# Selective scans: B written to DRAM with zeros between its values and read back as diagonal matrices for three of eight token tiles, the other five scaled on ScalarE

## The chip, the core and the metric

The program runs on one core of one Trainium2 chip. That core has TensorE (PE, with its weight loads shown as PEld), VectorE (DVE), ScalarE (ACT), GpSimd (POOL) and SyncE (SP). SP computes nothing here; it issues the DMAs of the scans, one after the other. The metric is the device time of one execution in microseconds (us), the median of several runs. Profiles are of one execution each.

## What is computed

The input is an image of 256 x 256 tokens with 128 channels. A triangle attention layer comes first, then a layer with a selective scan. Only the scans are touched here:

```python
def step(h, inp):
    d_t, x_t, B_t, C_t = inp
    dA = jnp.exp(d_t[..., None] * As)
    h = dA * h + (d_t * x_t)[..., None] * B_t[:, :, None, :]
    y = jnp.einsum('bkdn,bkn->bkd', h, C_t)
    return (h, y)
```

There are K = 4 scans over L = 65,536 tokens (along the rows and along the columns, each forwards and backwards). Every scan has D_INNER = 256 channels and D_STATE = 16 states, so for each state n the kernel needs, per channel and token, the decay `dA`, the input `d*x*B[n]`, the recurrence, and the product with `C[n]`.

## The kernel before

The function `scans` cuts each scan into 64 blocks of TB = 1024 tokens, so there are 256 blocks. A block has NJ = 8 token tiles of P = 128 tokens. The 256 channels are two halves (h = 0, 1). A block is worked off in 32 steps: s = 2m + h, with m the state. In each step

- `recur` (L853) runs one recurrence over 128 channels x 1024 tokens on DVE (L858). At h = 1 it also takes the last state (L863, DVE) and multiplies both halves by C on POOL (L865, two instructions), for which `cc`, one row of C spread over 128 partitions, has come by DMA.
- `turn` (L841) makes the input of the next step on PE. The product `d*x` is at hand as `dxt`, with tokens on partitions. The scan wants channels on partitions and the product with B[n], which is one number per token. So for tiles 0 to 3 PE multiplies `dxt` with a 128 x 128 matrix `dg` that has B on its diagonal (L846; an f32 product is two passes, so eight matmul records), and for tiles 4 to 7 it transposes `but`, which is `dxt` already multiplied by B (L848; four records). The result lies in one of two PSUM buffers `mm`, which alternate. A buffer is free when the DVE instruction that reads it has ended.
- `scale` (L830) makes what `turn` will need six steps later, on ACT: two `dg` (identity times B, L833) and two `but` (L835) per step. Both have rings of four, one buffer for each m modulo 4.
- `decay` (L837) makes exp(delta * A) on ACT for four steps later (L839), in a ring of six.
- `collect_some` (L882) turns the products with C back with PE transposes that accumulate in PSUM (the helper in L617), three states behind; `evict` (L893) adds them to y on DVE in steps 6 and 8 of the next block (L898).
- `fetch` (L825), at h = 1, has SP issue the DMA of the `cc` of state m + 4. It waits until POOL has done state m, which read the buffer before.

Beside its own steps a block prepares the next one: `begin` (L737) returns a list of pieces, each with a step and a mark for before or after that step's own work, and `advance` issues them. Steps 6, 8, 18 and 20 have `rate` (PE, L750, with a wait for a `mm` buffer); steps 6 to 12 have six wide activations on ACT (L759 to L774), steps 11 to 14 four instructions on POOL (`log1p` L780, `less` L777), steps 18 and 20 `softplus` on DVE (L783), steps 22 and 24 `turn_rate` (PE, L790) with `times_x` (DVE, L794). At the start of a block SP issues the next block's `bt` (B, 64 KB) and `xk` (1 MB); in step 8 it stores y (L902, 1 MB), in step 16 it loads the next y (L948, 1 MB), in step 21 it loads `dt` (32 KB).

The scans stand under `tc.manual_schedule()`, so every engine works off its instructions in the order in which the Python code issues them. The DMAs of the scans are all on SP's one queue: SP waits for whatever a DMA needs before it issues it, and what stands behind it on SP waits too. Eighteen blocks form the body of a hardware loop, which is run three times for each scan; the other ten blocks of a scan are written out.

Of the kernel before, what the change touches and what calls it, by code (L numbers as in the profile page):

```python
# [29 lines left out]
AF = mybir.ActivationFunctionType  # L30
# [5 lines left out]
P = 128  # L36
# [4 lines left out]
DI = 256  # L41
NH = DI // P
DS = 16
# [576 lines left out]
def scans(tc, io, c):  # L620
# [11 lines left out]
    nc = tc.nc  # L632
    TB = 1024
    NJ = TB // P
# [5 lines left out]
    with tc.tile_pool(name="e_w", bufs=1) as wp, tc.tile_pool(name="e_1", bufs=1) as sb1, tc.tile_pool(  # L640
# [11 lines left out]
        def ring(name, n, shape, pool=wp):  # L652
            return [pool.tile(shape, F32, name=f"{name}{i}") for i in range(n)]

        DJ = NJ // 2
        xks = ring("xk", 1, [P, NJ, DI])

        dts = ring("dt", 1, [P, TB])
# [4 lines left out]
        ybs = ring("yb", 1, [P, NJ, DI])  # L663
        ccs = ring("cc", 4, [P, TB])
        dgs = ring("dg", 4, [P, DJ, P])
        bus = ring("but", 4, [P, NJ - DJ, DI])
        das = ring("da", DA, [P, TB])
        hss = ring("hs", HS, [P, NH, TB])
        mms = ring("mm", 2, [P, TB], psum)
# [3 lines left out]
        def mm():  # L673
            count[0] += 1
            return mms[count[0] % 2]
# [9 lines left out]
        class Block:  # L685
# [40 lines left out]
            def load_tokens(self):  # L726
                nc.sync.dma_start(out=self.as_rows(self.bt), in_=self.rows(io["bk"][self.S.k]))
                nc.sync.dma_start(out=self.as_rows(self.xk), in_=self.rows(io["xk"]))

            def advance(self, now, after):  # L730
                if self.pieces is None:
# [5 lines left out]
        def begin(B):  # L737


            k = B.S.k  # L740
            B.pu, B.e = {}, None

            def rate(h):
                if B.e is None:
                    B.e = sb1.tile([P, NH, TB], F32, name="e")
                pu = B.pu[h] = mm()
                for q in range(0, TB, T):
                    nc.tensor.matmul(  # L750
                        pu[:, q : q + T],
                        dtw[0 : DR + 1, k, h * P : (h + 1) * P],
                        B.dt[0 : DR + 1, q : q + T],
                        start=True,
                        stop=True,
                    )

            def size(h):
                nc.scalar.activation(B.e[:, h, :], B.pu[h], AF.Abs)  # L759

            def exp():
                nc.scalar.activation(B.e, B.e, AF.Exp, scale=-1.0)

            def log():
                B.lw = sb1.tile([P, NH, TB], F32, name="lw")
                nc.scalar.activation(B.lw, B.e, AF.Ln, bias=1.0)  # L766

            def one_plus():
                B.w = sb1.tile([P, NH, TB], F32, name="w")
                nc.scalar.activation(B.w, B.e, AF.Identity, bias=1.0)  # L770

            def rest():

                nc.scalar.activation(B.w, B.w, AF.Identity, scale=-1.0, bias=1.0)  # L774

            def less(h):
                nc.gpsimd.tensor_tensor(B.lw[:, h, :], B.lw[:, h, :], B.w[:, h, :], ALU.add)  # L777

            def log1p(h):
                nc.gpsimd.tensor_tensor(B.lw[:, h, :], B.lw[:, h, :], B.e[:, h, :], ALU.add)  # L780

            def softplus(h):
                nc.vector.scalar_tensor_tensor(B.delta[:, h, :], B.pu[h], 0.0, B.lw[:, h, :], ALU.max, ALU.add)  # L783

            def turn_rate(i):
                B.pt = mm().rearrange("p (j d) -> p j d", d=DI)
                for j in range(NJ // 2):
                    for h in range(NH):
                        at = (i * NJ // 2 + j) * P
                        nc.tensor.transpose(B.pt[:, j, h * P : (h + 1) * P], B.delta[:, h, at : at + P], c.ident)  # L790

            def times_x(i):
                G = N // P
                nc.vector.tensor_tensor(  # L794
                    B.dxt[:, i * NJ // 2 : (i + 1) * NJ // 2, :].rearrange("p (w g) c -> p w g c", g=G),
                    B.pt.rearrange("p (w g) c -> p w g c", g=G),
                    B.in_order(B.xk, i, 2),
                    ALU.mult,
                )

            return [
                (6, False, rate, 0),
                (6, True, size, 0),
                (8, False, rate, 1),
                (8, True, size, 1),
                (9, True, exp),
                (10, True, log),
                (11, True, log1p, 0),
                (11, True, one_plus),
                (12, True, log1p, 1),  # L810
                (12, True, rest),
                (13, True, less, 0),
                (14, True, less, 1),

                (18, False, rate, 0),
                (18, True, softplus, 0),
                (20, False, rate, 1),
                (20, True, softplus, 1),
                (22, False, turn_rate, 0),
                (22, True, times_x, 0),  # L820
                (24, False, turn_rate, 1),
                (24, True, times_x, 1),
            ]

        def fetch(B, m):  # L825
            nc.sync.dma_start(out=ccs[m % 4], in_=B.S.C[m : m + 1, B.where()].partition_broadcast(P))

        def scale(B, m, h):  # L830
            dg, bu = dgs[m % 4], bus[m % 4]
            for j in range(h * DJ // 2, (h + 1) * DJ // 2):
                nc.scalar.activation(dg[:, j, :], c.ident, AF.Copy, scale=B.bt[:, B.slot(j), m : m + 1])  # L833
                at = B.slot(DJ + j)
                nc.scalar.activation(bu[:, j, :], B.dxt[:, DJ + j, :], AF.Copy, scale=B.bt[:, at, m : m + 1])  # L835

        def decay(B, m, h):  # L837
            da = das[((B.n * DS + m) * NH + h) % DA]
# [2 lines left out]
        def turn(B, m, h):  # L841
            d1 = B.d1 = mm()
            dg, bu = dgs[m % 4], bus[m % 4]
            hc = slice(h * P, (h + 1) * P)
            for j in range(DJ):
                nc.tensor.matmul(d1[:, j * P : (j + 1) * P], B.dxt[:, j, hc], dg[:, j, :], start=True, stop=True)  # L846
            for j in range(DJ, NJ):
                nc.tensor.transpose(d1[:, j * P : (j + 1) * P], bu[:, j - DJ, hc], c.ident)  # L848
            d1s.append(d1)

        d1s = []
# [56 lines left out]
        def body(blocks, before, after):  # L908
# [8 lines left out]
            def at(u):  # L917
                x, s = divmod(u, U)
                return (at_hand[x], *divmod(s, NH)) if x in at_hand else None

            def do(f, u):
                if at(u):
                    f(*at(u))

            if before is None:
                blocks[0].load()
                blocks[0].load_tokens()
                blocks[0].advance(U, True)
                blocks[0].free = set(range(NJ // PB))
                blocks[1].load()  # L930
                for m in range(4):
                    fetch(blocks[0], m)
                for u in range(3 * NH):
                    do(scale, u)
                for u in range(4):
                    do(decay, u)
                do(turn, 0)
            for x, B in enumerate(blocks):
                nxt = at_hand.get(x + 1)
                for s in range(U):  # L940
                    u = x * U + s
                    m, h = divmod(s, NH)
                    if s == 0 and nxt:
                        nxt.load_tokens()
                    if s == 21 and x + 2 in at_hand:
                        at_hand[x + 2].load()
                    if s == 16:
                        nc.sync.dma_start(out=B.as_rows(B.y), in_=B.rows(io["y"]))  # L948
                    if nxt:
                        nxt.advance(s, False)  # L950
                    recur(B, m, h)
                    do(turn, u + 1)
                    if at(u - LAG * NH):
                        waiting.extend((*at(u - LAG * NH), j) for j in range(NJ))
                    collect_some(len(waiting) if s == LAG * NH - 1 else share.get(s, 10))
                    if x - 1 in at_hand and s in (6, 8):
                        evict(at_hand[x - 1], B, (s - 6) // 2)
                    if nxt:
                        nxt.advance(s, True)
                    do(decay, u + 4)  # L960
                    if u == 0:
                        nc.scalar.preload_act_table_set("natural_log_exp_and_others")
                    do(scale, u + 3 * NH)
                    if h == NH - 1 and at(u + 1 + 3 * NH):
                        fetch(*at(u + 1 + 3 * NH)[:2])
            if not after:
# [9 lines left out]
        first = (n - passes * LOOP) // 4 * 2  # L976
# [21 lines left out]
def output(tc, io, c):  # L998
# [73 lines left out]
    "dc1": (KD // 2 * RC, NT),  # L1072
    "dcT": (KD // 2 * RC, NT),
    "y": (NT, DI),
}


# [56 lines left out]
```

## Time and profile before

| | |
|---|---|
| time, median of 3 runs | 28445.06 us (28438.65 to 28445.41) |
| the profiled execution, span | 28447.5 us |
| TensorE clock granted, mean | 0.965 |
| scans: L846 first at 4,768 us, last L858 at 27,653 us | some 22,890 us for 256 blocks, 89.4 each |
| busy share PE / DVE / ACT / POOL, whole span | 94% / 88% / 89% / 81% |
| DMA queue of the scans (q1) | 3339.77 MB, 34.6% of 16 engines |

The shares are means over the whole program: attention, convolution and output stand in them too. A share near the top says that an engine is rarely idle, and not that it sets the pace: an engine that waits a little at each step and one that is waited for look much alike there. What sets the pace is read from which engine has no gap in a stretch, and from what ends the gaps of the others. DMA rows give what moved and for how long; a row of the timeline gives start, length, engine, line and the instruction, with the idle time before it and what ended that in brackets.

### The profile page before, as it was taken

The numbers are of one execution on the slowest core, as the hardware profiler recorded it, in microseconds if no ns is written. First come the engines' busy times: TensorE is split into PE (matmuls) and PEld (weight loads), VectorE is DVE, ScalarE is ACT, GpSimd is POOL, SyncE is SP. The second block draws the span as 40 slices with busy tenths as digits, with TensorE's granted clock in tenths as the row PEclk, the third lists the DMA queues.
The fourth block names the chain that finished last, engine by engine and source line by source line (L and its number), as shares of the span: only waits on it lengthen the run. The fifth ranks groups of instructions, "written<-read, shape, count | busy, mean of one in ns | idle before, by whom it ended". The sixth has DMA issues, their size and how long they took to land. (4 is left out here: it accounts for less than half of the span.)

```text
span 28447.5 us, 528099 instructions
## 1 busy us (share of the span) xinstructions
PE 26610.1 (94%) x196490; PEld 22529.2 (79%) x196490; DVE 24922.2 (88%) x24253; ACT 25332.4 (89%) x49673; POOL 22944.4 (81%) x10118
## 2 busy tenths in 40 slices
PE   8999996999999999999999999999999999999998
PEld 3555444888888888888888888888888888888884
DVE  4777665999999999999999999999999999999987
ACT  6875224999999999999999999999999999999987
POOL 2443002999999999999999999999999999999983
PEclk9999998999999999999999999999999999999999
DMA  5112345433433333333334333333333333333335
GB/s 206 55 50 71 111 116 115 132 132 129 133 130 133 132 131 132 132 131 132 128 132 133 131 133 132 131 132 129 132 132 130 133 132 129 132 130 132 133 132 172
DMA packets 1923996, 3630.07 MB, mean 128 GB/s; under 512 B 532297, under 2 KB 1240009, under 8 KB 1889490
## 3 DMA queue, kind: packets, MB, share of 16 engines
q1 hardware_dynamic: 1424722, 3339.77, 34.6%
q10 hardware_dynamic: 496640, 255.88, 3.2%
q8 instruction: 1568, 25.69, 0.4%
q14 instruction: 1066, 8.73, 0.1%
HBM read 3002.42 MB, written 592.84 MB: 126 GB/s over the span
## 5 line engine op out<-in xcount | busy, mean ns | idle before, releaser
L865 POOL TENSOR_TENSOR hs<-hs,cc 128x1024 f32<-128x1024 f32 x8192 | 19202.5, 2380 | 1346.1 <-DVE state L863 679.9
L858 DVE TENSOR_TENSOR_SCAN hs<-da,state,mm 128x1024 f32<-128x1024 f32 x8192 | 18976.6, 2340 | 1465.4 <-PE mm L848 1074.7
L846 PE MATMUL mm<-dg,dxt 128*128 128x128 f32 x65536 | 9305.0, 287 | 1065.1 <-DVE hs L858 886.1
L846 PEld LDWEIGHTS mm<-dg,dxt 128*128 128x128 f32 x65536 | 8328.4, 199 | 2257.9 <-DVE hs L858 1897.8
L839 ACT ACTIVATE da<-delta,A 128x1024 f32<-128x1024 f32 x8192 | 9328.4, 1139 | 112.2 <-PEq L984 76.0
L617 PE MATMUL y<-ident,hs 128*128 128x128 f32 x65536 | 8511.4, 275 | 1.4 <-POOL hs L865 1.4
L835 ACT ACTIVATE but<-dxt,bt 128x256 f32<-128x256 f32 x16384 | 8150.2, 497 | 11.4 <-DVE dxt L794 11.4
L617 PEld LDWEIGHTS y<-ident,hs 128*128 128x128 f32 x65536 | 7494.1, 143 | 1.9 <-POOL hs L865 1.9
L833 ACT ACTIVATE dg<-ident,bt 128x128 f32<-128x128 f32 x16384 | 6393.1, 390 | 0.2
L848 PE MATMUL mm<-ident,but 128*128 128x128 f32 x32768 | 5092.5, 280 | 0.0
L848 PEld LDWEIGHTS mm<-ident,but 128*128 128x128 f32 x32768 | 4011.4, 146 | 0.0
L750 PE MATMUL mm<-dt,dtw 9*128 9x512 f32 x4096 | 2033.0, 615 | 265.9 <-DMA bt<-mid_bk 184.5
L385 POOL TENSOR_TENSOR an<-ex,rs 128x1024 f32<-128x1024 f32 x512 | 970.2, 1895 | 1024.5 <-PE tp L394 566.3
L780 POOL TENSOR_TENSOR lw<-lw,e 128x1024 f32<-128x1024 f32 x512 | 1207.7, 2384 | 336.3 <-ACT lw L766 336.3
L750 PEld LDWEIGHTS mm<-dt,dtw 9*128 9x128 f32 x4096 | 680.7, 184 | 959.5 <-issue 733.3
L500 POOL MEMSET pad<- 128x10 f32 x32 | 3.7, 117 | 1650.0 <-PE ps L537 1639.9
L777 POOL TENSOR_TENSOR lw<-lw,w 128x1024 f32<-128x1024 f32 x512 | 1202.9, 2375 | 0.0
L537 PE MATMUL ps<-pad,w 128*128 128x512 f32 x2048 | 954.8, 610 | 161.0 <-ACT xi L525 161.0
L372 ACT ACTIVATE ex<-sc,nm 128x256 f32<-128x256 f32 x2048 | 1013.7, 499 | 0.4
L759 ACT ACTIVATE e<-mm 128x1024 f32<-128x1024 f32 x512 | 524.7, 1025 | 522.1 <-PE mm L750 521.9
L355 DVE CUSTOM_DVE_ANT_0 sc<-ps,bias 128x256 f32<-128x256 f32 x2048 | 746.2, 421 | 117.3 <-PE ps L340 117.3
L394 PEld LDWEIGHTS tp<-ident,an 128*128 128x128 f32 x4096 | 467.5, 141 | 470.7 <-POOL an L385 235.1
(137 smaller groups left out, 18522.4 us busy)
## 6 DMA issues: line engine op xcount, KB each, us to landing
cc<-mid_dc SPq DMA_DIRECT2D x2048, 512.0 KB
cc<-mid_dcT SPq DMA_DIRECT2D x2048, 512.0 KB
xk<-mid_xk SPq DMA_DIRECT2D x256, 1024.0 KB
yb<-mid_y SPq DMA_DIRECT2D x256, 1024.0 KB
mid_y<-yb SPq DMA_DIRECT2D x256, 1024.0 KB
xt<-mid_xT SPq DMA_DIRECT2D x64, 1024.0 KB
mid_xk<-xk ACTq DMA_DIRECT2D x32, 2048.0 KB
mid_y<-y ACTq DMA_DIRECT2D x32, 2048.0 KB
```

Of the source, the lines that this page charges most:

```text
L372: nc.scalar.activation(exs[u][:, x, :], scs[u][:, e, jt, :], AF.Exp, scale=-1.0, bias=nms[u][:, e, jt : jt + 1], accum_out=sms[u][:, x : x ...
L617: nc.tensor.matmul(out, in_, c.ident, is_transpose=True, start=start, stop=stop, skip_group_check=True)
L750: nc.tensor.matmul(pu[:, q : q + T], dtw[0 : DR + 1, k, h * P : (h + 1) * P], B.dt[0 : DR + 1, q : q + T], start=True, stop=True,)
L777: nc.gpsimd.tensor_tensor(B.lw[:, h, :], B.lw[:, h, :], B.w[:, h, :], ALU.add)
L780: nc.gpsimd.tensor_tensor(B.lw[:, h, :], B.lw[:, h, :], B.e[:, h, :], ALU.add)
L833: nc.scalar.activation(dg[:, j, :], c.ident, AF.Copy, scale=B.bt[:, B.slot(j), m : m + 1])
L835: nc.scalar.activation(bu[:, j, :], B.dxt[:, DJ + j, :], AF.Copy, scale=B.bt[:, at, m : m + 1])
L839: nc.scalar.activation(da, B.delta[:, h, :], AF.Exp, scale=A[:, B.S.k * NH + h, m : m + 1])
L846: nc.tensor.matmul(d1[:, j * P : (j + 1) * P], B.dxt[:, j, hc], dg[:, j, :], start=True, stop=True)
L848: nc.tensor.transpose(d1[:, j * P : (j + 1) * P], bu[:, j - DJ, hc], c.ident)
L858: nc.vector.tensor_tensor_scan(o, d0, d1, state[:, m, h : h + 1], ALU.mult, ALU.add)
L865: nc.gpsimd.tensor_tensor(hs[:, x, :], hs[:, x, :], ccs[m % 4], ALU.mult)
```

## The change

- DJ, the number of tiles that are multiplied by a diagonal matrix, goes from 4 to 3 (tiles 0, 2, 4), and the tiles that are scaled on ACT from 4 to 5 (tiles 1, 3, 5, 6, 7).
- The diagonal matrices are no longer made by ACT. There is one SBUF tile `z` of 128 x 1664 f32, set to zero once. A new piece `spread`, in steps 10, 13, 16 and 19, has ACT copy 12 values of B per partition (four states, three tiles) of the next block into `z`, 128 elements apart, and has SP store the whole of `z` (832 KB) in a DRAM scratch area `apart`, which has room for two blocks.
- A new function `diagonal` has SP load one state's three matrices (128 x 384 f32, 192 KB) from there, row p starting one element earlier than a straight copy would, so that the value of row p falls on column p. It is issued at h = 0, for the state that `turn` uses from six steps later.
- `scale` issues two or three `but` activations per step and no `dg`. `turn` has six records of L846's kind and five of L848's.

```diff
-        DJ = NJ // 2
+        DJ = 3
+        BJ = NJ - DJ
+        by_diagonal, by_scale = (0, 2, 4), (1, 3, 5, 6, 7)
+        GS = 4
+        ZL = P * (GS * DJ + 1)
...
-        bus = ring("but", 4, [P, NJ - DJ, DI])
+        bus = ring("but", 4, [P, BJ, DI])
+        zs = ring("z", 1, [P, ZL])
+        for z in zs:
+            nc.vector.memset(z, 0.0)
...
+            def apart(self, g):
+                return io["apart"][self.b % 2, g]
...
-            return [
+            def spread(g):
+                z = zs[0]
+                first, step = B.slot(by_diagonal[0]), B.slot(by_diagonal[1]) - B.slot(by_diagonal[0])
+                nc.scalar.copy(
+                    z[:, P - 1 : P - 1 + GS * DJ * P].rearrange("p (m j q) -> p j m q", j=DJ, q=P)[:, :, :, 0],
+                    B.bt[:, first : first + step * (DJ - 1) + 1 : step, g * GS : (g + 1) * GS],
+                )
+                nc.sync.dma_start(out=B.apart(g), in_=z)
+
+            pieces = [(10 + 3 * g, True, spread, g) for g in range(DS // GS)]
+            return sorted(pieces + [
...
-            ]
+            ], key=lambda x: x[:2])
...
+        def diagonal(B, m):
+            of = B.apart(m // GS)
+            of = bass.AP(of.tensor, of.offset + P - 1 + m % GS * DJ * P, ((ZL - 1, P), (1, DJ * P)))
+            nc.sync.dma_start(out=dgs[m % 4].rearrange("p j q -> p (j q)"), in_=of)
...
-            dg, bu = dgs[m % 4], bus[m % 4]
-            for j in range(h * DJ // 2, (h + 1) * DJ // 2):
-                nc.scalar.activation(dg[:, j, :], c.ident, AF.Copy, scale=B.bt[:, B.slot(j), m : m + 1])
-                at = B.slot(DJ + j)
-                nc.scalar.activation(bu[:, j, :], B.dxt[:, DJ + j, :], AF.Copy, scale=B.bt[:, at, m : m + 1])
+            bu = bus[m % 4]
+            for x in range(h * BJ // 2, (h + 1) * BJ // 2):
+                j = by_scale[x]
+                nc.scalar.activation(bu[:, x, :], B.dxt[:, j, :], AF.Copy, scale=B.bt[:, B.slot(j), m : m + 1])
...
-            for j in range(DJ):
-                nc.tensor.matmul(d1[:, j * P : (j + 1) * P], B.dxt[:, j, hc], dg[:, j, :], start=True, stop=True)
-            for j in range(DJ, NJ):
-                nc.tensor.transpose(d1[:, j * P : (j + 1) * P], bu[:, j - DJ, hc], c.ident)
+            for x, j in enumerate(by_diagonal):
+                nc.tensor.matmul(d1[:, j * P : (j + 1) * P], B.dxt[:, j, hc], dg[:, x, :], start=True, stop=True)
+            for x, j in enumerate(by_scale):
+                nc.tensor.transpose(d1[:, j * P : (j + 1) * P], bu[:, x, hc], c.ident)
...
+                for m in range(3):
+                    diagonal(blocks[0], m)
...
                     do(scale, u + 3 * NH)
+                    if h == 0 and at(u + 3 * NH):
+                        diagonal(*at(u + 3 * NH)[:2])
                     if h == NH - 1 and at(u + 1 + 3 * NH):
                         fetch(*at(u + 1 + 3 * NH)[:2])
...
+    "apart": (2, 4, P, P * 13),
```

In the built program SP's order around the middle of a block is: `cc` (step 9), store of `z`, `dg` of state 8, `cc` (11), `dg` 9, store of `z`, `cc` (13), `dg` 10, `cc` (15), load of y, store of `z`, `dg` 11, `cc` (17), `dg` 12, store of `z`, `cc` (19), `dg` 13. A block has 41 DMAs on SP, against 21 before.

## The prediction, made before the changed kernel was run

> **What bounds the kernel now.** I looked first at the costliest groups of the page, then at one block of the steady part of a scan, whole and engine by engine, and last at SP and the DMAs in it. The groups:
>
> ```profile
> L865 POOL TENSOR_TENSOR hs<-hs,cc 128x1024 f32<-128x1024 f32 x8192 | 19202.5, 2380 | 1346.1 <-DVE state L863 679.9
> L858 DVE TENSOR_TENSOR_SCAN hs<-da,state,mm 128x1024 f32<-128x1024 f32 x8192 | 18976.6, 2340 | 1465.4 <-PE mm L848 1074.7
> L839 ACT ACTIVATE da<-delta,A 128x1024 f32<-128x1024 f32 x8192 | 9328.4, 1139 | 112.2 <-PEq L984 76.0
> L835 ACT ACTIVATE but<-dxt,bt 128x256 f32<-128x256 f32 x16384 | 8150.2, 497 | 11.4 <-DVE dxt L794 11.4
> L833 ACT ACTIVATE dg<-ident,bt 128x128 f32<-128x128 f32 x16384 | 6393.1, 390 | 0.2
> ```
>
> A step costs POOL 2.38 and DVE 2.34 us, and the change touches neither row; it takes work from ACT. So is ACT what the others wait for? One block, 88.79 us long:
>
> ```profile
> core 0: us, PE busy (x) PEld busy (x) DVE busy (x) ACT busy (x) POOL busy (x), PEclk, DMA share, GB/s
> 15000.00:15088.79 88.79, 84.27 (x674) 76.80 (x673) 82.70 (x57) 86.73 (x167) 84.07 (x37) 0.98 0.41 133
> ```
>
> ACT is the fullest engine, but being full isn't being waited for. DVE's order of time decides it (start, length, instruction, idle time before it and what ended that):
>
> ```profile
> 15012.39 2.35 DVE L858 TENSOR_TENSOR_SCAN hs<-da,state,mm 128x1024 f32<-128x1024 f32 x1 [0.31 <-PE y L617]
> ...
> 15017.83 2.35 DVE L858 TENSOR_TENSOR_SCAN hs<-da,state,mm 128x1024 f32<-128x1024 f32 x1 [1.98 <-PE mm L848]
> ...
> 15026.85 2.35 DVE L858 TENSOR_TENSOR_SCAN hs<-da,state,mm 128x1024 f32<-128x1024 f32 x1
> 15029.12 1.20 DVE L794 TENSOR_TENSOR dxt<-mm,xk 128x1024 f32<-128x1024 f32 x1
> 15030.96 2.35 DVE L858 TENSOR_TENSOR_SCAN hs<-da,state,mm 128x1024 f32<-128x1024 f32 x1 [0.64 <-PE mm L848]
> ...
> 15040.01 4.58 DVE L858 TENSOR_TENSOR_SCAN hs<-da,state,mm 128x1024 f32<-128x1024 f32 x2
> ```
>
> These are steps 18, 19, 22, 23 and 26 to 27 (counted from the two evictions, which are steps 6 and 8). In plain steps DVE runs without a gap. Its gaps come after the pieces, where a piece holds the second mm buffer and `turn` can start only when the recurrence before has ended. In this block DVE waits 4.2 us for PE (5 times) and 0.8 for ACT (twice). DVE with those gaps is the chain; POOL (36 instructions of about 2.35) has 4.7 us to spare, ACT 2.1. So ACT's relief can bring little, and the question is what the new DMAs bring late. For that, POOL and SP in the same block:
>
> ```profile
> 14993.01 9.47 POOL L865 TENSOR_TENSOR hs<-hs,cc 128x1024 f32<-128x1024 f32 x4 [1.91 <-DVE state L863]
> 15002.41 4.74 POOL L780 TENSOR_TENSOR lw<-lw,e 128x1024 f32<-128x1024 f32 x2
> 15007.08 4.73 POOL L865 TENSOR_TENSOR hs<-hs,cc 128x1024 f32<-128x1024 f32 x2
> 15011.74 4.70 POOL L777 TENSOR_TENSOR lw<-lw,w 128x1024 f32<-128x1024 f32 x2
> 15016.38 23.36 POOL L865 TENSOR_TENSOR hs<-hs,cc 128x1024 f32<-128x1024 f32 x10
> ```
>
> ```profile
> 15002.51 18.95 SPq L826 DMA_DIRECT2D cc<-mid_dc  x3
> 15021.78 0.38 SPq L948 DMA_DIRECT2D yb<-mid_y  x1
> 15025.78 4.99 SPq L826 DMA_DIRECT2D cc<-mid_dc  x2
> ```
>
> The reader is to see that SP goes at POOL's pace: each `cc` waits for POOL to finish a state (in this block SP waits for POOL 73.8 us in all). At step 10 POOL is on DVE's heels (it waited 1.91). The four instructions of the softplus then put it four steps behind: it ends state 7, step 15, at 15021.05, while DVE is in step 20. Only then does SP issue the `cc` of step 15 and, 0.7 us on, the load of y of step 16.
>
> **The change, part by part.**
>
> *ACT.* From one start to the next a `dg` takes 0.29 us and a `but` 0.40 in the timeline. Per step two `dg` go and half a `but` comes: 0.58 - 0.20 = 0.38 us less, 12 us a block. This lies beside DVE's chain; it is worth at most the 0.8 us that DVE waited for ACT. Behind the 0.64 of these (step 25) stands a wait for PE of the same kind as at step 23, so I take 0.25. The four `spread` copies have no row; between a DVE instruction of 2 elements (0.16) and a `dg` (0.39) I take 0.3 each, 1.2 us in a block where ACT has over 12 to spare.
>
> *PE.* A `turn` of 12 records takes 1.36 us from its first weight load to the end of its last; with 11 it takes 0.11 less. That counts where DVE waits for it: steps 7, 9, 23, 25 outside the stretch below, 0.44 a block.
>
> *The wait that is added.* `turn` now waits for a DMA. Behind it on PE stand all collects and the next `turn`, so DVE stops with it. The loads are issued behind `cc`, hence at POOL's pace, and where POOL is latest they are latest. For state 11: SP's order is `cc` (15), y, the store of z, `dg` 11, all within two us of 15021.05. The rows show that one queue's transfers follow each other: no packet of the `cc` issued at 15025.78 starts before 15026.8, when y begins to end. Bytes ahead and including: 0.52 + 1.05 + 0.85 + 0.20 = 2.62 MB. What the first two take is measured:
>
> ```profile
> DMA packets 1105, 1.52 MB, mean 253 GB/s; under 512 B 17, under 2 KB 975, under 8 KB 1104
> ```
>
> That is 15021.05 to 15027.05, with the first packets at 15022.1; the packet records of 32 such places have y landed about 5.7 us after its issue (5.3 to 6.9), here 15027.5. The last slices of this window run at 355 to 410 GB/s, so 1.05 MB of z and `dg` take 2.8 us, and I add 0.6 for the slowest of the 16 engines and the semaphore: 15030.9. Before, the `turn` of step 22 started at 15024.45; it is held 6.5 us.
>
> The Trainium skill, DMA: Bandwidth & Descriptors, Specifications, gives about 358 GB/s of HBM per core; by that figure 2.62 MB take an estimated 7.3 us after the first packet, 15029.4, and the whole sum would be some 380 us lower. The measured 253 to 306 GB/s for the mixed part decide.
>
> *The cold PE.* In those 6.5 us PE has nothing to do.
>
> ```profile
> 15024.45 1.06 PE L846 MATMUL mm<-dg,dxt 128*128 128x128 f32 x8
> 15025.35 0.60 PE L848 MATMUL mm<-ident,but 128*128 128x128 f32 x4
> ```
>
> ```profile
> 4783.14 2.08 PE L846 MATMUL mm<-dg,dxt 128*128 128x128 f32 x8 [7.39 <-DVE hs L858]
> 4785.01 1.06 PE L848 MATMUL mm<-ident,but 128*128 128x128 f32 x4
> 4785.86 1.92 PE L846 MATMUL mm<-dg,dxt 128*128 128x128 f32 x8
> ```
>
> After 7.39 us idle a `turn` takes 2.53 instead of 1.36, and the next is slow too; all gaps of 4.4 us or more in the scans' steady part show this. The Trainium skill, TensorE: Matmul & The Clock Gate, Part 1, says that PE falls to half its clock after an idle window of about 3.4 us and needs as long to recover; the row agrees. So the `turn` takes 2.32 with 11 records, and step 22 starts at 15030.9 + 2.3 + 0.2 = 15033.4 against 15026.85: **+6.55**. `turn_rate` and the collects behind are slow for some 2 us more, which reaches `times_x` and step 23: 1.05 us less the cover of about half: **+0.5**.
>
> *The other loads.* State 3's `dg` (issued at step 0) stands behind `cc`, bt and the 1 MB of xk. xk lands 6.4 us after its issue and `turn` 6 starts 5.5 after; with 0.9 for `dg` and its semaphore it is 1.8 late, of which DVE, busy with step 5, feels **+0.9**. The loads of states 8, 9, 10, 12 and 13 I cost at nothing: each lands 0.3 to 4 us before its `turn`. The cover is the two to three steps (2.37 each) between POOL's end of a state and the `turn`; if transfers ran at half the speed, state 8 (behind a store) would cost 3 us and state 10 the same.
>
> *z, one buffer.* `spread` at steps 13, 16 and 19 waits for the store before. The last is the closest: it waits for the store of step 16 until about 15030.5, and behind it on ACT stands the `decay` of step 23, done by 15032. Step 23 now starts after 15038. Cost nothing, by cover of 6 us; SP stands at the store of step 19 until then, with `cc` 13 and `dg` 13 behind it, needed 10 us later.
>
> *Load on the DMA engines.* q1's 3339.77 MB in 34.6% of 16 engines is 21 GB/s for an engine; 4 x 0.85 + 16 x 0.2 = 6.6 MB more a block are 19 us of the 16 engines in some 96. Their share goes from 0.41 to about 0.58: no bound of its own.
>
> *Sum per block:* 6.55 + 0.5 + 0.9 - 0.25 - 0.44 = **+7.25 us**. Times 255 blocks 1850, and once some 20 us at the start, where four spreads of one z follow each other (4 x 5). 28447.5 + 1870 = 30317; the median lies 2.4 below its profiled run: **30315 us**, 6.6% slower.
>
> Bounds: if `dg` lands at 15029.4 and PE stays warm (step 22 at 30.9, +4.0), state 3 costs nothing, and all 0.8 of ACT and 1.2 of gaps come back, that is +4.0 - 2.0 a block, 28975. If z and `dg` move at half the rate (2.8 more), state 3 costs 1.5, the clock stays low long enough for another microsecond and nothing is gained: 6.55 + 0.5 + 2.8 + 1.5 + 1 = +12.35, 31615.
>
> **The rivals.**
>
> 1. *Faster: the loads are there in time.* If DMAs of one queue don't hold each other up, or POOL reaches state 7 over 6 us earlier, then only gaps shrink: 7 waits x 0.11 + 0.25 to 0.8, some 1.3 us a block, 28110; at the utmost down to POOL's 84.07 of 88.79, 27240. For it: POOL's 4.7 us to spare. Against: these lie in steps 6 to 9, and the softplus comes after. It decides from `dg` 11 landing before 15025. Chance 0.09.
> 2. *Slower by more: the round trip of z.* Reads with a pitch of 6652 bytes and rows of 1536 have no like in the trace, nor does a store that the next `spread` waits for. Past 6 us more per store, ACT's `decay` is late, then every `spread` but the first stalls DVE: at 2 us for each of three on top of the sum, +13.25, 31840. For it: nothing measured; against: y, in 1024-byte packets, moves at 46 ns each, the same 22 GB/s per engine as larger ones. Chance 0.11.
> 3. *No change:* loads 1.4 us late at one place, paid by the gaps, 28445. Needs `dg` 11 five us earlier. Chance 0.03.
>
> **How the numbers follow.** The forecast has 0.77; with rival 2 it makes 0.88 for slower by over 0.2%, the difference that a measurement of this kernel can tell; rival 1 and a little of 3 make faster 0.09, same 0.03. The range leaves out the faster cases and the far end of rival 2: 29250 (+3.1 a block) to 31450.
>
> **What would show it.** On PE the largest wait before L870 (the diagonal product) is for a DMA, once a block and about 6 us long, at step 22; the `turn` after it is at half speed; DVE's gap there is about 7 us and its other gaps are 0.1 shorter. POOL's idle time rises by 7 us a block, ACT's by about 18. I am wrong if PE waits for no DMA, if the long wait stands at another state, or if ACT's wait for z is what DVE waits for.

## The result and the profile after

| | before | changed kernel |
|---|---|---|
| time, median | 28445.24 us (4 runs) | 31225.97 us (31215.01 to 31338.04, 4 runs) |
| ratio of the means | | 1.0987, 95% interval 1.097 to 1.1004 |
| profiled execution, span | 28447.5 us | 31336.2 us |
| granted TensorE clock | 0.965 | 0.922 |

The kernel became 9.9% slower. The forecast was 30315 us; the time lies in its range, 911 us above the point. The groups that matter, from the page of the changed kernel (busy time, mean ns of one, idle time before it and what ended most of that):

```profile
L889 POOL TENSOR_TENSOR hs<-hs,cc 128x1024 f32<-128x1024 f32 x8192 | 19178.5, 2368 | 4255.3 <-PE y L617 2574.7
L882 DVE TENSOR_TENSOR_SCAN hs<-da,state,mm 128x1024 f32<-128x1024 f32 x8192 | 18960.0, 2340 | 4141.8 <-PE mm L872 3832.3
L870 PE MATMUL mm<-dg,dxt 128*128 128x128 f32 x49152 | 7788.0, 298 | 3800.8 <-DMA dg<-mid_apart 2876.7
L863 ACT ACTIVATE da<-delta,A 128x1024 f32<-128x1024 f32 x8192 | 9358.1, 1142 | 696.0 <-DVE hs L882 391.1
L814 ACT COPY z<-bt 128x12 f32<-128x12 f32 x1024 | 206.8, 202 | 3379.7 <-DMA mid_apart<-z 3379.7
```

No recurrence and no product on POOL became slower. What grew is idle time: DVE's before its recurrence by 2676 us (1465.4 to 4141.8), nearly the whole loss, PE's before the diagonal product to 3801, three quarters of it ended by the DMA of `dg`. There is a second large wait, ACT's for z (3380 us), and the page doesn't tell what either of the two would cost alone. The order of time in one block shows where they lie. DVE, at steps 20 to 23:

```profile
15029.89 2.35 DVE L882 TENSOR_TENSOR_SCAN hs<-da,state,mm 128x1024 f32<-128x1024 f32 x1
...
15033.96 2.35 DVE L882 TENSOR_TENSOR_SCAN hs<-da,state,mm 128x1024 f32<-128x1024 f32 x1 [0.19 <-PE mm L872]
15036.34 0.16 DVE L887 TENSOR_REDUCE state<-hs 128x2 f32<-128x2 f32 x1
15045.34 2.35 DVE L882 TENSOR_TENSOR_SCAN hs<-da,state,mm 128x1024 f32<-128x1024 f32 x1 [8.84 <-PE mm L872]
15047.60 1.20 DVE L804 TENSOR_TENSOR dxt<-mm,xk 128x1024 f32<-128x1024 f32 x1
15049.33 2.35 DVE L882 TENSOR_TENSOR_SCAN hs<-da,state,mm 128x1024 f32<-128x1024 f32 x1 [0.53 <-PE mm L872]
```

SP's issues in the same stretch, and then PE's and ACT's rows with their waits:

```profile
15031.83 0.34 SPq L846 DMA_DIRECT2D cc<-mid_dc  x1
15032.50 0.39 SPq L974 DMA_DIRECT2D yb<-mid_y  x1
15033.00 0.53 SPq L818 DMA_DIRECT2D mid_apart<-z  x1
15033.62 0.67 SPq L851 DMA_DIRECT2D dg<-mid_apart  x1
```

```profile
15032.37 0.94 PE L870 MATMUL mm<-dg,dxt 128*128 128x128 f32 x6
15033.15 0.71 PE L872 MATMUL mm<-ident,but 128*128 128x128 f32 x5
...
15042.55 1.62 PE L870 MATMUL mm<-dg,dxt 128*128 128x128 f32 x6 [8.37 <-DMA dg<-mid_apart]
15043.96 1.27 PE L872 MATMUL mm<-ident,but 128*128 128x128 f32 x5
...
15088.03 1.62 PE L870 MATMUL mm<-dg,dxt 128*128 128x128 f32 x6 [3.85 <-DMA dg<-mid_apart]
15089.45 1.27 PE L872 MATMUL mm<-ident,but 128*128 128x128 f32 x5
15090.52 1.91 PE L617 MATMUL y<-ident,hs 128*128 128x128 f32 x8
15092.36 3.78 PE L760 MATMUL mm<-dt,dtw 9*128 9x512 f32 x4
```

```profile
15042.26 0.21 ACT L814 COPY z<-bt 128x12 f32<-128x12 f32 x1 [12.59 <-DMA mid_apart<-z]
```

`cc`, y, z and state 11's `dg` are issued within 2 us of 15031.83, when POOL ends state 7, and the `turn` of step 22 starts at 15042.55, 10.05 us after the issue of y. Its records take almost twice as long as those at 15032.37, and step 22 starts 2.8 us after that. State 3's load holds PE for 3.85 us at step 6, and there too PE is slow afterwards: the `rate` of step 6 takes 3.78 us instead of the 1.98 that it takes at step 20 of the same block, so step 7 is late as well. ACT is released at 15042.26, 0.3 us before PE: the two long waits end together, and what one of them alone is worth had to be tried.

Per step, over 240 blocks of each profiled run, the mean time from the start of one recurrence to the next (us; steps that differ by under 0.1 everywhere are left out; the labels are those of the experiments below):

```
step   before  after    e1     e2     e3     e4     e5     e6     e7     e8     e9
 6      2.46   4.03   3.73   3.76   2.47   3.97   2.47   2.46   2.47   2.47   2.47
 7      4.18   5.13   4.83   4.87   4.43   4.90   4.27   4.30   4.24   4.69   4.44
 8      2.49   2.50   2.50   2.50   2.50   2.50   2.50   2.85   2.50   2.50   2.50
 9      4.58   4.25   4.25   4.28   4.42   4.23   4.36   5.11   4.44   4.18   4.34
16      2.62   2.57   2.48   2.58   2.47   2.56   2.47   2.79   2.54   2.47   2.58
17      2.37   2.27   2.28   2.29   2.26   2.27   2.26   2.26   2.28   2.26   2.29
18      2.51   2.47   2.47   2.47   2.47   2.47   2.46   2.60   2.47   2.46   2.48
19      4.69   4.35   4.47   4.41   4.40   4.41   4.34   4.60   4.32   4.31   4.13
20      2.49   2.52   2.53   2.53   2.58   2.51   2.53   2.51   2.55   2.66   2.57
21      4.57   4.22   4.20   4.20   4.33   4.17   4.35   4.21   4.20   4.34   4.21
22      2.47  12.43   9.15  12.25   2.46   8.08   2.46   2.46   2.46   2.46   2.46
23      4.10   4.29   4.29   4.27   7.86   4.27   3.99   3.99   3.88   3.99   3.88
24      2.46   2.47   2.47   2.46   2.47   2.47   4.99   2.46   4.00   2.46   2.47
25      4.11   3.99   3.99   3.99   4.02   3.99   4.14   4.00   3.97   3.99   3.87
block  89.37 100.72  96.85 100.06  92.30  96.02  90.82  89.81  89.53  88.45  87.89
```

A block is 11.35 us longer, times 256 is 2906; the spans differ by 2889 (the profiled execution is the slowest of the four, 112 us above the median). So this table holds the whole result: +9.96 at step 22, +2.52 at steps 6 and 7, and some 0.3 less at each of steps 9, 19 and 21.

### The profile page after: what moved, and what is told of

The parts are those of the page before. It is cut to its first block, busy times and chain, and to the rows that moved or that the text cites. A ratio compares the mean times of both kernels' runs of the same rounds, so it can differ in the third digit from the quotient of the medians.

```text
span 31336.2 us, 512207 instructions
## 1 busy us (share of the span) xinstructions
PE 26760.7 (85%) x188298; PEld 22327.3 (71%) x188298; DVE 24976.7 (80%) x24254; ACT 22589.5 (72%) x38409; POOL 22919.1 (73%) x10118
## 5 line engine op out<-in xcount | busy, mean ns | idle before, releaser
L882 DVE TENSOR_TENSOR_SCAN hs<-da,state,mm 128x1024 f32<-128x1024 f32 x8192 | 18960.0, 2340 | 4141.8 <-PE mm L872 3832.3
L870 PE MATMUL mm<-dg,dxt 128*128 128x128 f32 x49152 | 7788.0, 298 | 3800.8 <-DMA dg<-mid_apart 2876.7
L870 PEld LDWEIGHTS mm<-dg,dxt 128*128 128x128 f32 x49152 | 6561.5, 203 | 5301.8 <-issue 2897.2
L859 ACT ACTIVATE but<-dxt,bt 128x256 f32<-128x256 f32 x20480 | 8964.1, 495 | 3.5 <-DVE dxt L804 3.2
L617 PE MATMUL y<-ident,hs 128*128 128x128 f32 x65536 | 8800.3, 281 | 2.2 <-POOL hs L889 1.9
L617 PEld LDWEIGHTS y<-ident,hs 128*128 128x128 f32 x65536 | 7794.8, 147 | 3.1 <-POOL hs L889 2.4
L872 PE MATMUL mm<-ident,but 128*128 128x128 f32 x40960 | 6228.7, 286 | 0.0
L872 PEld LDWEIGHTS mm<-ident,but 128*128 128x128 f32 x40960 | 5124.8, 149 | 0.0
L814 ACT COPY z<-bt 128x12 f32<-128x12 f32 x1024 | 206.8, 202 | 3379.7 <-DMA mid_apart<-z 3379.7
L760 PE MATMUL mm<-dt,dtw 9*128 9x512 f32 x4096 | 2128.2, 640 | 274.1 <-DMA bt<-mid_bk 185.3
```

Source lines behind the costliest of these rows:

```text
L617: nc.tensor.matmul(out, in_, c.ident, is_transpose=True, start=start, stop=stop, skip_group_check=True)
L760: nc.tensor.matmul(pu[:, q : q + T], dtw[0 : DR + 1, k, h * P : (h + 1) * P], B.dt[0 : DR + 1, q : q + T], start=True, stop=True,)
L859: nc.scalar.activation(bu[:, x, :], B.dxt[:, j, :], AF.Copy, scale=B.bt[:, B.slot(j), m : m + 1])
L872: nc.tensor.transpose(d1[:, j * P : (j + 1) * P], bu[:, x, hc], c.ident)
L882: nc.vector.tensor_tensor_scan(o, d0, d1, state[:, m, h : h + 1], ALU.mult, ALU.add)
```

## The experiments

Three theories were to be told apart. Queue: `dg` is late because of what stands ahead of it on SP's queue when POOL is latest. z: ACT's wait for its one z holds up the `decay` behind it. Traffic: 6.6 MB more per block cost by themselves.

**One thing moved at a time.** e1 has ACT issue the stores, e2 moves the last filling of z, e4 moves the load of y.

```diff
 e1  -                nc.sync.dma_start(out=B.apart(g), in_=z)
     +                nc.scalar.dma_start(out=B.apart(g), in_=z)
 e2  -            pieces = [(10 + 3 * g, True, spread, g) for g in range(DS // GS)]
     +            pieces = [((10, 13, 16, 25)[g], True, spread, g) for g in range(DS // GS)]
 e4  -                    if s == 16:
     +                    if s == 17:
                              nc.sync.dma_start(out=B.as_rows(B.y), in_=B.rows(io["y"]))
```

> The four stores of z are issued by ACT, which made the copy, and not by SP; nothing else differs from the changed kernel. Queue theory (the load of state 11's diagonals is late because it stands on SP's queue behind cc, y and z): z no longer stands ahead of it on that queue, is stored some 10 us earlier than at POOL's pace, so the load lands 2.4 us earlier; the gap before step 22 falls from 12.4 to about 10 us start to start, the one before step 6 stays (4.0), time about 30500 to 30650. z theory (what counts is that ACT waits for the store before it may fill z again): ACT's longest wait of 12 us goes, and most of the 2780 us with it, under 29300. Traffic theory (the bytes are too many whatever their order): same bytes, 31100 to 31350.

> The fourth filling of z and its store move from step 19 to step 25, where the store before is long done; nothing else differs from the changed kernel. z theory: ACT no longer waits 12 us for z, and the time falls by most of 2780 us, under 29300. Queue theory: that wait lay beside the wait for the load, nothing that DVE waits for goes: 31100 to 31350, the gap before step 22 stays at 12.4 us. Traffic theory: the same.

> The load of y (1 MB) moves from step 16 to step 17, that is behind the load of state 11's diagonals on SP's queue and ahead of the next cc; nothing else differs from the changed kernel. Queue theory: 1.05 MB less ahead of that load, 3 to 4 us earlier; the gap before step 22 falls from 12.4 to about 9 us, 30200 to 30450; a sum of separate prices. z theory: the store of z is done 3 us earlier too, so the same fall can't tell it from the queue theory here. Traffic theory: 31100 to 31350.

Measured: e1 30367.38 us (ratio to before 1.0677, 1.0656 to 1.0698), step 22 at 9.15; e2 31200.12 (1.097, 1.0948 to 1.0992), step 22 at 12.25; e4 30114.67 (1.0588, 1.0567 to 1.0609), step 22 at 8.08. With z or y out of the way of state 11's load step 22 comes 3.3 or 4.4 us earlier; the time falls by 859 and 1111 us. That is more than the bytes alone explain (0.85 and 1.05 MB take an estimated 2.1 to 2.4 and 2.6 to 3.0 us at the 355 to 410 GB/s that the prediction read; in e1 y also lands a microsecond sooner, see the last section), and both times lie some 100 us below the ranges expected. In e2 ACT's wait for z is gone, and DVE gains nothing:

```profile
DVE hs L882 <- PE mm L872: 2251.3, 905, 12.3
ACT da L863 <- DVE hs L882: 2176.3, 1252, 11.0
...
PE mm L870 <- DMA dg<-mid_apart: 1770.2, 362, 11.8
```

These are waits of e2 between 9,000 and 25,000 us (total us, times, longest). ACT now waits for DVE instead of for z; PE still waits for `dg`. z is not what paces the changed kernel, and traffic is at most a part of it, since e4 wins 1111 us with the same bytes.

e1 also bears on a rule. The Trainium skill, DMA: Bandwidth & Descriptors, Issuing engines are not separate DMA queues, says that DMAs of several engines run on the same 16 DMA engines, and that issuing on more than one saves only the time it takes the sequencer to issue them. Here more than that goes, 859 us with the same bytes: in a block of e1, ACT issues the store of step 16 at 15005.32, 6.3 us before SP issues the load of y at 15011.65, so it isn't ahead of `dg` when that is wanted. ACT isn't free in e1, though: the store of step 19 and the `decay` behind it wait for DMAs that SP issued, and ACT stands idle for 8.82 us there.

**Loading earlier.** e3 loads each state's diagonals two steps sooner; `dg` is free by then, since the `turn` that read the buffer last has been issued.

```diff
-                for m in range(3):
+                for m in range(4):
                     diagonal(blocks[0], m)
...
-                    if h == 0 and at(u + 3 * NH):
-                        diagonal(*at(u + 3 * NH)[:2])
+                    if h == 0 and at(u + 4 * NH):
+                        diagonal(*at(u + 4 * NH)[:2])
```

> Each state's diagonals are loaded two steps earlier in the program (for the turn eight steps later instead of six; four instead of three states are loaded ahead at the start); ring, bytes and stores are as in the changed kernel. Queue theory: state 11's load then stands behind the cc of step 13 and not behind that of step 15, y and z, and lands some 9 us earlier; state 3's no longer behind xk. The gaps before steps 22 and 6 fall from 12.4 and 4.0 us to 2.5 each, what is left of the change is the smaller gaps (0.1 to 0.7 us at six places): 28000 to 28300, below the kernel before. z theory: ACT still waits for z, over 30000. Traffic theory: over 30000.

Measured: 29191.82 us (1.0266, 1.0249 to 1.0283). Steps 22 and 6 are back at 2.46, as the queue theory had it, and 2034 of 2780 us are gone. But the time lies 900 us above what was expected: step 23 takes 7.86. Its rows:

```profile
15006.94 0.21 ACT L814 COPY z<-bt 128x12 f32<-128x12 f32 x1 [13.23 <-DMA mid_apart<-z]
15007.05 1.15 ACT L863 ACTIVATE da<-delta,A 128x1024 f32<-128x1024 f32 x1
...
15008.23 2.35 DVE L882 TENSOR_TENSOR_SCAN hs<-da,state,mm 128x1024 f32<-128x1024 f32 x1 [4.28 <-ACT da L863]
```

Here is z's wait after all: the store of step 16, still behind y at POOL's pace, holds ACT for 13 us, `decay` of step 23 is late, and DVE waits 4.28 us for it. In the changed kernel this wait lay under the longer one. And e3 hides the next: at 15007.46 PE had waited 2.55 us for state 12's diagonals, for the `turn` of step 24 (2.7 us on the mean), while DVE stood still for ACT anyway.

**Both at once, then nothing large at step 16.** e5 has the early loads and the last store at step 25. e8 also moves the third store from step 16 to 19 and the load of y from 16 to 28; all bytes stay.

```diff
 e5  = e3, and
     +            pieces = [((10, 13, 16, 25)[g], True, spread, g) for g in range(DS // GS)]
 e8  = e3, and
     +            pieces = [((10, 13, 19, 25)[g], True, spread, g) for g in range(DS // GS)]
     -                    if s == 16:
     +                    if s == 28:
                              nc.sync.dma_start(out=B.as_rows(B.y), in_=B.rows(io["y"]))
```

> Both edits at once: the diagonals are loaded two steps earlier, and the fourth filling and store of z go to step 25. Stores, loads and bytes per block are those of the changed kernel. Theory of two covers (the wait for the load and the wait for z lie side by side, and each alone would hold DVE at step 22 or 23): the 3.8 us that step 23 still lost with the early loads alone go, every step is at most as long as before the change; 92.3 - 3.8 = 88.5 us a block against 89.4, that is 28150 to 28300, below the kernel before by 0.5 to 1%. Traffic theory (what was left in the early-load run is contention by the additional bytes): no further fall, 29100 to 29250.

> As the run with both edits (early loads, last store at step 25), but the load of y moves from step 16 to step 28 and the third filling and store of z from step 16 to step 19, so that nothing large stands in the queue at step 16, where POOL is latest. Bytes as in the changed kernel. Queue theory: the 2.5 us that step 24 waited there for state 12's load go; every step is at most as long as before the change, about 88.3 us a block against 89.4: 28100 to 28300. Traffic theory: the additional 6.6 MB per block cost by themselves, 28700 to 28850 as before this edit.

e5: 28799.43 us (1.0124, 1.0109 to 1.014), a miss by some 500. Step 23 is back at 3.99, but step 24 takes 4.99: the wait that e3 had already, and that the expected sum left out. By the new order it is state 12's load that follows y and z in step 16, and PE waits for it at the `turn` of step 24:

```profile
15022.64 0.91 PE L870 MATMUL mm<-dg,dxt 128*128 128x128 f32 x6 [1.71 <-DMA dg<-mid_apart]
```

The queue had moved to the next state. e8, with y and z away from there: 28250.08 us, ratio 0.9932 (0.9918 to 0.9945). Steps 22 to 25 are all at or below those of before; of the others step 7 is longer by 0.5 and step 20 by 0.2, against what was expected, and why was not looked into. The same traffic at a higher rate is now no hindrance. Between 12,000 and 18,000 us, first the kernel before, then e8 (busy times in the order of the head of the windows view; then the clock, DMA share and GB/s):

```profile
12000.00:18000.00 6000.00, 5704.52 (x45145) 5211.57 (x45144) 5559.86 (x3761) 5835.89 (x11154) 5656.92 (x2419) 0.97 0.39 131
...
12000.00:18000.00 6000.00, 5631.44 (x43449) 5049.21 (x43448) 5615.51 (x3804) 5174.01 (x8283) 5701.37 (x2444) 0.97 0.63 207
```

The DMA share is 0.63 against 0.39 in that stretch before, and the kernel is 0.7% faster than before. As an account of the loss, the traffic theory falls.

**What the split itself is worth, and two tiles.** e6 is the kernel before with tiles 0, 2, 4 by diagonal and five scaled, all made by ACT. e7 and e9 are e5 and e8 with two tiles by diagonal (z is 128 x 1152).

```diff
 e6  (kernel before)
     -        DJ = NJ // 2
     +        DJ = 3
     +        by_diagonal, by_scale = (0, 2, 4), (1, 3, 5, 6, 7)
     ...
     -                nc.scalar.activation(dg[:, j, :], c.ident, AF.Copy, scale=B.bt[:, B.slot(j), m : m + 1])
     +            for x in range(h * DJ // 2, (h + 1) * DJ // 2):
     +                nc.scalar.activation(dg[:, x, :], c.ident, AF.Copy, scale=B.bt[:, B.slot(by_diagonal[x]), m : m + 1])
     ...
     +            for x in range(h * len(by_scale) // 2, (h + 1) * len(by_scale) // 2):
     +                j = by_scale[x]
     +                nc.scalar.activation(bu[:, x, :], B.dxt[:, j, :], AF.Copy, scale=B.bt[:, B.slot(j), m : m + 1])
     ...
 e7  = e5, e9 = e8, and
     -        DJ = 3
     +        DJ = 2
     -        by_diagonal, by_scale = (0, 2, 4), (1, 3, 5, 6, 7)
     +        by_diagonal, by_scale = (0, 2), (1, 3, 4, 5, 6, 7)
     -    "apart": (2, 4, P, P * 13),
     +    "apart": (2, 4, P, P * 9),
```

> The kernel before with the split alone: tiles 0, 2, 4 by diagonal matrices and five by scaled copies, but ACT makes the diagonals, with no z and no DMA for them. PE has 11 records per turn instead of 12; ACT has 3 x 0.29 + 5 x 0.40 = 2.87 us per state instead of 2.76, 88.6 us a block in all, as much as DVE's chain needs. If the shorter turn is the whole gain of the change: 28150 to 28300. If ACT's relief is needed for it: ACT now paces and the time is 28400 to 28800.

> As the run with both edits, with two tiles by diagonals from DRAM (0, 2) and six scaled by ACT: z is 128 x 1152, a state's load 128 KB; PE has 10 records per turn, ACT 2.40 us per state instead of 2.00, some 81 us a block. If the gaps at the six places with a piece are one turn long minus the piece, each falls by another 0.11 us: 0.66 a block, 170 us below the run with three tiles, 27950 to 28150. If ACT's or DMA's share in those gaps counts, no difference to it.

> The same with two tiles by diagonals from DRAM and six scaled by ACT. Queue theory: the 1.5 us of step 24 in the two-tile run go, and the turn of 10 records takes 0.1 off each of four to six gaps: 88.0 us a block, 28000 to 28200. Traffic theory: 28450 to 28550.

Measured: e6 28563.94 us (1.0037, 1.0024 to 1.0051); e7 28512.75 (1.0027, 1.0016 to 1.0039), a miss, with step 24 at 4.00 for e5's reason; e9 28066.02 (0.9867, 0.9852 to 0.9882), the fastest, 1.3% under the kernel before. In e6 ACT is busy 5917 of 6000 us (from 12,000 to 18,000), and steps 8, 9, 16 and 18 grow together by 1.2 us, which undoes the 0.7 us that steps 19 to 25 gain: without relief for ACT the shorter `turn` is worth nothing. With relief and one record less, steps 23 and 25 of e9 are at 3.88 and 3.87, 0.11 to 0.12 below e8.

## Why the prediction was right, and where it was mis-sized

- *The chain is DVE's, and ACT's relief brings little.* Right. With the long new waits gone (e8), a block is 0.92 us shorter than before. e6 adds what the prediction didn't say: that little needs the relief.
- *SP at POOL's pace.* Right: from the end of step 11 to the issue of y it takes 24.34 us (mean) in both kernels.
- *State 11's load is late at step 22.* Right in place and cause, shown by e1, e3 and e4. The price from the end of step 11 to step 22 was put at 6.55; the means are 28.89 and 37.98, 9.1 us. Three shares: the load released PE 10.84 us after the issue of y and not 9.1 (1.7 us; in the scans along the rows the last packet of y came 7.7 us after its issue, where the sum had y landed after 5.7, and even in the kernel before it was 6.5 on the mean); the cold `turn` and its hand-over took 2.8 and not 2.5; and the block that the sum was made on had step 22 half a microsecond later than the mean.
- *Cold PE.* Right: after 8.37 us idle the six and five records took 1.62 and 1.27 us in the rows above, against 0.94 and 0.71 in a warm `turn` of the same kernel. What it adds at step 23 was put at 0.5; step 23 is 0.2 longer than before, and 0.3 longer than in e6 and e8, which have the shorter `turn` at full speed.
- *State 3's load, +0.9.* The place was right, the size was not: +2.52. This is the term that failed most in proportion. The lateness itself was put too low (step 6: 1.57), and it was not counted that PE is cold there as well and the `rate` of step 6 stands behind the `turn`: step 7 takes 0.95 more. The prediction had made that step of thought for step 22 alone. So PE's long wait for `dg` comes twice in a block, and not once as its signs had it.
- *z costs nothing, by cover.* Right while the cover lasts (e2), and the cover was named. What lay beneath was 3.8 us (e3).
- *Smaller gaps, -0.69.* Outside the stretch -0.45 (steps 9 and 25). The -0.9 of steps 16 to 21 is lost, as POOL's pace and not DVE's sets step 22.
- *DMA no bound of its own.* Right: e8, at a share of 0.63, where the changed kernel has 0.55 in the same stretch.

By the same sum with the measured terms: 9.1 + 0.2 + 2.5 - 0.45 = 11.35 us a block, against 7.25. The mechanism held; two terms, step 22's and state 3's, were too small by 2.5 and 1.6 us. These misses add up and don't cancel, and the time lies 224 us below the upper end of the range.

## What to carry to other kernels

A small load that many wait for comes after what stands ahead of it on its queue (here 10.84 us after the issue of a 1 MB load), and a queue whose waits follow a late engine is late as a whole: before work is turned into DMAs, look up what stands ahead of each at the step where its issuer is furthest behind, and issue it before that. Waits can lie side by side; taking away the longer one shows the next, so a sum of prices holds only with the cover named. And a long wait of PE costs more than its length: after 3.85 and 8.37 us of idle time what followed ran at about half speed, after the 1.71 us in e5 (0.91 us for six records) it didn't.

## What was not expected of the hardware

- Rows read with a pitch of 6652 bytes, 4 bytes off from one to the next, showed no extra cost (the same rows at an aligned pitch were not run): packets of 1536 bytes took 65 ns and z's of 6656 bytes 253 ns, 24 and 26 bytes per ns, against 22 for y's of 1024 bytes (46 ns).
- A large store right behind a load on the same queue made the load later. In the scans along the rows the last packet of y came 7.5 to 7.7 us after its issue in the four runs with the store of z directly behind it (the changed kernel, e2, e3, e5), and 6.5 to 6.7 us in the four without (the kernel before, e1, e6, e8). In e1 `dg` stands directly behind y, and y comes at 6.7, so it is the store and not `dg`. In the block of the changed kernel shown above, the packets of the first 2 us of y's load took 99 to 129 ns, instead of 46 to 57 in the block of before; on the mean over the blocks the first packets differ far less, and how the store holds up the load stays open.
